# The down product turned round: bf16 passes on bare 4-bit weights, and norm products on either of two engines

## The chip, the cores and the metric

The kernel runs on one core of a Trainium2 chip. The core has five engines, each with its own instruction queue that is worked off strictly in order: TensorE (PE, matrix products; PEld is its weight load), VectorE (DVE), ScalarE (ACT), GpSimd (POOL) and SyncE (SP, which here only starts DMA transfers). They meet through semaphores. The metric is device microseconds (us) of one launch, taken as the median of several runs; smaller is better. Beside the timed runs there is one profiled execution, from which every line of the trace comes.

## The reference

A batch of 16 sequences, 512 tokens of width 512, goes through one attention block and one feed-forward block:

```python
x = x + layernorm(attention(layernorm(x)))      # 16 heads of 32, low-rank q and kv, ALiBi, causal
x = x + layernorm(ffn(layernorm(x)))

def ffn(x):                                     # I = 1408
    w_gu   = fp4_values(gate_up_packed) * scale # [2*I, 512], one scale per 128 inputs and output row
    w_down = fp4_values(down_packed) * scale    # [512, I], one scale per 128 inputs and output row
    gate, up = split(x @ w_gu.T)
    y = (silu(gate) * up) @ w_down.T
    return y / sqrt(mean(y * y) + 1e-6)
```

The weights of the feed-forward block come as 4-bit floating-point values, eight to a 32-bit word, with an fp16 scale for each group of 128 inputs. The 4-bit values (0, 0.5, 1, 1.5, 2, 3, 4, 6 and their negatives) are exact in bf16; the scaled ones are not.

## The kernel before, in words

**Order of the work.** The function builds a list of tasks (`task`, line 77). A task has the engines that may run it, with a cost for each, a due time, and the buffers it reads, writes or holds. `Plan.run` (line 120) then lays all tasks out with a list scheduler: it takes the task that can start first, then the one with the earlier due time, among those due within a window of 0.5 (one unit is one batch) of the next PE task. The result is one fixed order for each engine; nothing is decided on the chip. A task on PE is allowed to start 350 ns after its inputs by the plan's costs. Buffers come from small pools (`SLOTS`, line 270): eight PSUM banks, two `g`, two `u`, two `sum`, two `th` and so on, and a buffer is free again after its last reader in the plan. The plan runs several batches interleaved: while the feed-forward block of batch b is computed, the attention of b+1 and b+2 is.

**Feed-forward block** (`ffn`, line 841). For each of the NI = 11 groups of 128 hidden units, gate and up are computed transposed (hidden units on partitions, 512 tokens along the free side). The normalized input was split in `tail` into three bf16 parts whose sum is the f32 value (`x2`, lines 822 to 833). For each of four input chunks, one PSUM bank gets three bf16 matmuls (one for each part) with the bare 4-bit values as weights (line 859); the bank is scaled as it is read, by ACT (line 873) or by DVE, which also adds (line 880), since the group scale is one number per partition here. POOL adds the two halves (line 886), ACT takes a tanh (line 893), DVE makes the gate (line 896), and POOL multiplies by up into `hT` (line 900), in f32.

The down product then takes `hT` as weights and the scaled f32 `w_dn` as the moving side: for each of four blocks of 128 tokens, 11 f32 matmuls of 128x512 add up in one bank (line 908), so that the result has tokens on partitions:

```python
nc.tensor.matmul(pm.t, h_t.t[:, i, t * P : (t + 1) * P], w_dn.t[:, i, :], ...)
```

Mean and variance of the bank are taken on DVE (`stats`, lines 425 and 426; lines 930 and 931), the root on POOL (lines 446 and 447), and DVE writes the normalized `z` from the bank (line 940). POOL adds it to x (line 945) and starts the store (line 948).

**Norms.** `norm` (line 430) is used three times for a block of tokens: on the input (`xl`), on the attention output read from the bank `pw`, and on x before the feed-forward block. Each ends in a DVE product with mean and root (line 439). With line 940 that is four such products for each of 64 blocks, all on DVE.

**Unpacking** happens once, in the plan of batch 0 (`unpack`, line 489). A DMA copies the words of a group eightfold to partitions, two DVE instructions shift and mask them in place (line 510) in `w_dn`'s own memory. For gate and up, ACT then turns them into bf16 (line 520) and SP stores them to DRAM (`w_gu`), from where each batch loads them again. For down, DVE multiplies with the scales (line 534), which an extra DMA per group brought to all partitions.

Of the kernel before, what the change touches and what calls it, by code (L numbers as in the profile page):

```python
# [12 lines left out]
I32 = mybir.dt.int32  # L13
# [221 lines left out]
def attn_ffn_kernel(  # L235
# [36 lines left out]
        "xl": (NT, [P, D], F32),  # L272
        "x": (2 * NT - 1, [P, D], F32),
        "xnT": (1, [P, ND, L], F32),
# [8 lines left out]
        "x2": (1, [P, 3, ND, L], BF16),  # L283
        "hT": (1, [P, NI, L], F32),
        "g": (2, [P, L], F32),
        "u": (2, [P, L], F32),
        "sum": (2, [P, L], F32),
        "th": (2, [P, L], F32),
# [72 lines left out]
    def load_xl(b, t):  # L361
        xl = xls[b, t] = buf("xl", f"xl_{b}_{t}")
        task(
            {SP: dma(2.6)},
            lambda e: nc.sync.dma_start(xl.t, x_in[b, t * P : (t + 1) * P, :]),
            b - 0.6 + 0.05 * t, writes=[xl],
        )
# [30 lines left out]
    gu = Buf(None, None, "w_gu")  # L398
    w_dn = fixed([P, NI, D], "w_dn")

# [3 lines left out]
    s_gu = fixed([P, NI * NGU], "s_gu")  # L404
    task({SP: dma(3.0)}, lambda e: nc.sync.dma_start(raw.t.bitcast(F16)[:, : NI * NGU], gus), -0.34, writes=[raw])

    def make_scales(e):
        nc.gpsimd.tensor_scalar(s_gu.t, raw.t.bitcast(F16)[:, : NI * NGU], 1.0, None, ALU.mult)
        ups = s_gu.t.rearrange("p (i c) -> p i c", c=NGU)[:, :, ND:]
        nc.gpsimd.tensor_scalar(ups, ups, 0.5, None, ALU.mult)  # L410

    task({POOL: (700.0, 800.0)}, make_scales, 0.1, reads=[raw], writes=[s_gu])


# [15 lines left out]
    def norm(dst, src, rd, wr, tag, due, dur):  # L430

        st, mv, f = stats(src, tag, due)
        task({DVE: (700.0 + 150, 1000.0)}, f, due, reads=rd, writes=[st, mv])
        r = tiny(1, f"r_{tag}")
        task({POOL: (800.0, 900.0)}, lambda e: rsqrt(r.t, mv.t[:, 1:2], EPS_LN), due,
             reads=[mv], writes=[r])
        task(
            {DVE: dur},
            lambda e: nc.vector.tensor_scalar(
                dst(), src(), mv.t[:, 0:1], r.t, ALU.subtract, ALU.mult  # L440
            ),
            due, reads=[mv, r, *rd], writes=wr,
        )

# [42 lines left out]


    def unpack(packed, rows, cols, at, due):
        n = cols // D  # L490
        words = [(w_dn, at + k) for k in range(n)]
        ap = lambda: w_dn.t[:, at : at + n, :].bitcast(I32).rearrange("p i n -> p (i n)")

# [8 lines left out]
            ),  # L502
            due, writes=words,
        )
        for args in (
            (shl, None, ALU.logical_shift_left),
            (3, -0x72000000, ALU.arith_shift_right, ALU.bitwise_and),
        ):
            task({DVE: dve(cols, -0.15 * cols)},
                 lambda e, args=args: nc.vector.tensor_scalar(ap(), ap(), *args),  # L510
                 due, reads=words, writes=words)
        high = lambda: ap().bitcast(F16).rearrange("p (n two) -> p n two", two=2)[:, :, 1]
        return words, high

    def unpack_gate_up(i):
        due = 0.15 + 0.06 * i
        wi = buf("th", f"wq_{i}")
        words, high = unpack(gup, i * 16, NGU * P, i % (NI // 2) * 2, due)
        task({ACT: act(NGU * P)},
             lambda e: nc.scalar.activation(wi.t.bitcast(BF16), high(), AF.Copy, scale=2.0**14),  # L520
             due, reads=words, writes=[wi])
        task({SP: dma(2.0)}, lambda e: nc.sync.dma_start(w_gu[i], wi.t.bitcast(BF16)), due,
             reads=[wi], writes=[(gu, i)])

    def unpack_down(i):
        due = 0.85 + 0.06 * i
        sc = buf("y", f"sc_{i}")
        task({SP: dma(3.5)},
             lambda e: nc.sync.dma_start(sc.t.bitcast(F16)[:, :D], dns[i : i + 1, :].to_broadcast([P, D])),
             due, writes=[sc])  # L530
        words, high = unpack(dnp, i * 16, D, i, due)
        task(
            {DVE: dve(D)},
            lambda e: nc.vector.scalar_tensor_tensor(
                w_dn.t[:, i, :], high(), 2.0**14, sc.t.bitcast(F16)[:, :D], ALU.mult, ALU.mult
            ),
            due, reads=[*words, sc], writes=words,
        )

# [3 lines left out]
    def first_norm(b, t):  # L543
        due = b - 0.3 + 0.06 * t
        if t == 0:
# [292 lines left out]

    GU, DN = 0.0074, 0.0079

    def ffn(m):
        b = m.b
        h_t = buf("hT", f"hT_{b}")
        at = b + FIRST + STEP * (NG * NT + 6.5)
        for i in range(NI):
# [4 lines left out]
            for half, kind in enumerate("gu"):  # L850
                acc = buf(kind, f"{kind}_{b}_{i}")
                add = buf("sum", f"{kind}2_{b}_{i}")
                for c in range(ND):
# [23 lines left out]
                    else:  # L877
# [21 lines left out]
            task({POOL: pool2(512)},  # L899
                 lambda e, i=i, th=th, u=u: nc.gpsimd.tensor_tensor(  # L900
                     h_t.t[:, i, :], th.t, u.t, ALU.mult),
                 at, reads=[th, u], writes=[(h_t, i)])
        for t in range(NT):
            pm = buf("bank", f"py_{b}_{t}")
            for i in range(NI):
                task(
                    {PE: pe(858)},
                    lambda e, i=i, t=t, pm=pm: nc.tensor.matmul(  # L908
                        pm.t,
                        h_t.t[:, i, t * P : (t + 1) * P],  # L910
                        w_dn.t[:, i, :],
                        start=i == 0,
                        stop=i == NI - 1,
                    ),
                    at, reads=[(h_t, i), (w_dn, i)], writes=[pm],
                )
                at += DN
            st, mv, f = stats(lambda pm=pm: pm.t, f"y_{b}_{t}", at)
# [7 lines left out]
            def g1(e, f=f, mv=mv, rr=rr):  # L926
                f(e)
                mean, var = mv.t[:, 0:1], mv.t[:, 1:2]
                ms, ri = rr.t[:, 0:1], rr.t[:, 1:2]
                nc.vector.scalar_tensor_tensor(ms, mean, mean, var, ALU.mult, ALU.add)  # L930
                nc.vector.scalar_tensor_tensor(ri, ms, EPS_LN, var, ALU.mult, ALU.add)

            task({DVE: (1100.0, 1300.0)}, g1, at, reads=[pm], writes=[st, mv, rr])
            task({POOL: (800.0, 900.0)},
                 lambda e, rr=rr: rsqrt(rr.t[:, 1:2], rr.t[:, 1:2], EPS_LN * EPS_RMS),
                 at, reads=[rr], writes=[rr])
            z, x = buf("th", f"z_{b}_{t}"), m.x[t]
            task(
                {DVE: dve(512, 80)},
                lambda e, z=z, pm=pm, mv=mv, rr=rr: nc.vector.tensor_scalar(  # L940
                    z.t, pm.t, mv.t[:, 0:1], rr.t[:, 1:2], ALU.subtract, ALU.mult),
                at, reads=[pm, mv, rr], writes=[z],
            )
            task({POOL: pool2(512)},
# [101 lines left out]
```

## Time and profile before

| | |
|---|---|
| median of 3 runs | 2723.1 us (2720.8 to 2723.44) |
| profiled execution | 2730.41 us, of which 2728.6 us from the first to the last instruction (its span) |
| mean granted TensorE clock in it | 0.992 |
| PE busy | 2653.2 us |
| DVE busy | 1977.7 us |
| ACT busy | 1364.1 us |
| POOL busy | 1190.2 us |

A busy time is the union of an engine's instructions. For PE it is rougher than for the others, because matmuls overlap in a pipeline and their ends are modelled; the distance from one matmul's start to the next is the better measure of what one costs, and a run of many back to back gives it. In lists of groups, a line has: code line, engine, operation, tiles written and read, shape, count, then busy us and mean ns of one, then the engine's idle time just before such instructions and what ended it.

### The profile page before, as it was taken

The page shows a single profiled execution, that of the slowest core. Times are in us where ns is not written, and L with a number is a line of the kernel's source. Part 1 is how long each engine was busy: PE and PEld are TensorE (multiplying, and loading weights), DVE is VectorE, ACT ScalarE, POOL GpSimd, SP SyncE. Part 2 cuts the span into 40 slices and gives each one's busy share as a digit, 9 for nine tenths or more (in the row PEclk, how much of TensorE's full clock was granted, in tenths as well). Part 3 has the DMA queues.
Part 4 walks back from the last instruction along what each step waited for, and adds up shares of the span by engine and source line. Part 5 has one row for each costly group of instructions (what it writes and reads, how often), then busy time and mean ns, then how long its engine had stood idle before and what let it go on. Part 6 is the DMA issues. An engine that isn't in the chain of part 4 may idle for free.

```text
span 2728.6 us, 44045 instructions
## 1 busy us (share of the span) xinstructions
PE 2653.2 (97%) x14733; PEld 1205.7 (44%) x14904; DVE 1977.7 (72%) x4446; ACT 1364.1 (50%) x3339; POOL 1190.2 (44%) x1328
## 2 busy tenths in 40 slices
PE   7989999999999999999999999999999999999998
PEld 3544444444444444444444444444444444444443
DVE  4887795958868587685866868678686876867673
ACT  5755372644636455363553635546364563645441
POOL 1044453535444354453534435354443544534474
PEclk9999999999999999999999999999999999999999
DMA  6577475674956649375584856738576484846710
GB/s 203 159 179 191 136 208 138 178 188 129 233 130 187 174 144 223 113 194 158 158 214 112 210 147 184 192 107 224 151 195 173 139 212 132 207 130 169 187 39 19
DMA packets 460177, 448.20 MB, mean 164 GB/s; under 512 B 38576, under 2 KB 380464, under 8 KB 452272
## 3 DMA queue, kind: packets, MB, share of 16 engines
q1 hardware_dynamic: 454832, 428.61, 59.6%
q0 software_dynamic: 5120, 16.78, 1.7%
q8 instruction: 118, 1.93, 0.3%
q14 instruction: 107, 0.88, 0.1%
HBM read 267.28 MB, written 178.00 MB: 163 GB/s over the span
## 4 chain that ended last, share of the span: by engine, by line
PE 85%; DMA 10%; DVE 2%; SPq 1%; ACT 1%; issue 1%; POOL 0%; POOLq 0%; DVEq 0%; ACTq 0%
PE py L908 22%; PE pu L859 14%; PE pg L859 13%; PE pw L803 8%; PE pq L561 7%; DMA pT<-pd 7%; PE s L641 6%; PE po L775 6%; PE pv L561 2%; PE pc L561 2%; PE pk L561 2%; DMA pd<-p 1%; PE ptf L455 1%; DMA w_dn<-gup 1%; SPq L755 1%
## 5 line engine op out<-in xcount | busy, mean ns | idle before, releaser
L908 PE MATMUL py<-w_dn,hT 128*128 128x512 f32 x1408 | 698.5, 606 | 0.1
L668 ACT ACTIVATE p<-p,nmx 128x128 f32<-128x128 f32 (+3 forms) x1024 | 564.2, 553 | 255.1 <-DVE nmx L653 234.5
L859 PEld LDWEIGHTS <-wi 128*128 128x128 bf16 x4224 | 402.7, 98 | 584.8 <-issue 168.9
L653 DVE CUSTOM_DVE_ANT_0 p<-s,dist 128x128 f32<-128x128 f32 (+3 forms) x1024 | 442.8, 486 | 157.8 <-PE s L641 155.1
L859 PE MATMUL pu<-x,wi 128*128 128x512 bf16 x2010 | 516.3, 382 | 7.5 <-issue 1.1
L859 PE MATMUL pg<-x,wi 128*128 128x512 bf16 x2043 | 498.7, 380 | 4.4 <-POOL x L831 0.9
L886 POOL TENSOR_TENSOR u<-u,u 128x512 f32<-128x512 f32 x176 | 242.5, 1378 | 487.9 <-DVE u L880 487.1
L748 DVE STREAM_TRANSPOSE p<-p 128x512 f32<-128x512 f32 x240 | 360.0, 1501 | 42.8 <-ACT p L668 42.7
L908 PEld LDWEIGHTS py<-w_dn,hT 128*128 128x128 f32 x1408 | 248.2, 190 | 247.1 <-issue 227.5
L880 DVE SCALAR_TENSOR_TENSOR u<-pu,s_gu,u 128x512 f32<-128x512 f32 x352 | 258.7, 743 | 125.3 <-ACT u L873 73.3
L873 ACT ACTIVATE u<-pu,s_gu 128x512 f32<-128x512 f32 x352 | 240.6, 685 | 214.3 <-PE pu L859 204.4
L880 DVE SCALAR_TENSOR_TENSOR g<-pg,s_gu,g 128x512 f32<-128x512 f32 x352 | 258.7, 740 | 96.0 <-ACT g L873 50.7
L873 ACT ACTIVATE g<-pg,s_gu 128x512 f32<-128x512 f32 x352 | 240.0, 683 | 144.3 <-PE pg L859 126.5
L886 POOL TENSOR_TENSOR g<-g,g 128x512 f32<-128x512 f32 x176 | 233.9, 1329 | 143.5 <-DVE g L880 142.3
L900 POOL TENSOR_TENSOR hT<-th,u 128x512 f32<-128x512 f32 x176 | 224.9, 1278 | 95.4 <-DVE th L896 89.8
L561 PE MATMUL pq<-xnT,w_q 128*128 128x512 f32 x512 | 233.3, 598 | 1.5 <-ACT w_q L416 1.5
L803 PE MATMUL pw<-w_o,atT 128*128 128x512 f32 x512 | 230.2, 593 | 0.0
L775 PE MATMUL po<-pT,v 128*32 128x128 f32 x5120 | 193.5, 278 | 30.5 <-DMA pT<-pd 28.9
L641 PE MATMUL s<-kT,qT 32*128 32x128 f32 (+3 forms) x2048 | 216.2, 487 | 1.8 <-ACT qT L583 1.7
L775 PEld LDWEIGHTS po<-pT,v 128*32 128x32 f32 x5120 | 125.8, 109 | 159.8 <-issue 98.0
L668 ACT ACTIVATION_READ_ACCUMULATOR p<-p,nmx 128x1 f32 x1024 | 194.6, 190 | 0.0
L803 PEld LDWEIGHTS pw<-w_o,atT 128*128 128x128 f32 x512 | 97.0, 190 | 122.7 <-issue 119.7
(87 smaller groups left out, 2341.4 us busy)
## 6 DMA issues: line engine op xcount, KB each, us to landing
pd<-p SPq DMA_DIRECT2D x60, 1024.0 KB
pT<-pd SPq DMA_DIRECT2D x240, 256.0 KB
pd<-p SPq DMA_DIRECT2D x60, 768.0 KB
pT<-pd SPq DMA_DIRECT2D x240, 192.0 KB
wi<-w_gu SPq DMA_DIRECT2D x176, 256.0 KB
pd<-p SPq DMA_DIRECT2D x60, 512.0 KB
pT<-pd SPq DMA_DIRECT2D x240, 128.0 KB
xl<-x_in SPq DMA_DIRECT2D x64, 256.0 KB
```

Of the source, the lines that this page charges most:

```text
L561: nc.tensor.matmul(pm.t, lhs(c), rhs(c), start=c == 0, stop=c == n - 1)
L641: nc.tensor.matmul(s[j].t[:, :w], q.t[rows, qb * P : (qb + 1) * P], k.t[rows, :w], start=True, stop=True,)
L653: lambda e, j=j: nc.vector.tensor_tensor_reduce(part(m, p, j), runs(s[j].t[:, :w]), runs(dist.t[:, L - w :]), -SLOPES[g * HPG + j], 3.4e38 ...
L668: lambda e, j=j: nc.scalar.activation(part(m, p, j), part(m, p, j), AF.Exp, bias=nmx.t[:, j : j + 1], scale=-1.0, accum_out=sums.t[:, qb * ...
L748: task({DVE: dve(row, 0.07 * row)}, lambda e: nc.vector.transpose(flat(p.t), flat(p.t)), due, reads=[p], writes=[p])
L775: nc.tensor.matmul(po.t[j * HD : (j + 1) * HD, qb * P : (qb + 1) * P], m.v.t[:, kb, h * HD : (h + 1) * HD], p_t.t[:, kb, :, j, :], start=k ...
L803: nc.tensor.matmul(pm.t, m.at.t[:, g, t * P : (t + 1) * P], w_o.t[:, g, :], start=g == 0, stop=g == NG - 1,)
L859: nc.tensor.matmul(pm.t, wi.t[:, o * P : (o + 1) * P], m.x2.t[:, n, c, :], start=n == 0, stop=n == 2,)
L873: lambda e, to=to, pm=pm, s=s: nc.scalar.activation(to.t, pm.t, AF.Copy, scale=s),
L880: lambda e, to=to, pm=pm, s=s: nc.vector.scalar_tensor_tensor(to.t, pm.t, s, to.t, ALU.mult, ALU.add),
L886: lambda e, acc=acc, add=add: nc.gpsimd.tensor_tensor(acc.t, acc.t, add.t, ALU.add),
L908: lambda e, i=i, t=t, pm=pm: nc.tensor.matmul(pm.t, h_t.t[:, i, t * P : (t + 1) * P], w_dn.t[:, i, :], start=i == 0, stop=i == NI - 1,),
```

## The change

The down product is done like gate and up. The output is kept transposed: for each hidden group i and each of four blocks of 128 outputs, one bank takes three bf16 matmuls, with the bare 4-bit values of `w_dn` (now bf16) as weights and the three bf16 parts of the hidden values (`h3`) as the moving side. `split` makes those parts from `u` in four steps: cast (ACT or DVE), subtract (DVE or POOL), cast, subtract. A bank no longer adds over i; it is scaled as it is read and added to `acc` in SBUF: by ACT for i = 0, by DVE with the sum in one instruction for odd i, by ACT to a buffer and then a POOL add for the other even i. When all 11 groups are in, `acc` is turned back by f32 transposes on PE into a bank for each block of tokens, and the norm follows as before.

The products at the end of all norms may be done by DVE or by ACT (`scaled`); for ACT a POOL instruction more (`shift`) makes minus mean times root. Unpacking uses two buffers of the pool `acc`, ACT makes the bf16 values for down as well, its due time is earlier, and its scales come in one DMA instead of eleven. Pools: `hT` is gone; `acc` (2) and `h3` (2) are new, `u` has 3, `sum` 4, `x` 8. The first norm and its load have earlier due times.

```diff
-        "x": (2 * NT - 1, [P, D], F32),
+        "x": (2 * NT, [P, D], F32),
...
-        "hT": (1, [P, NI, L], F32),
+        "acc": (2, [P, ND, L], F32),
+        "h3": (2, [P, 3, L], BF16),
-        "u": (2, [P, L], F32),
-        "sum": (2, [P, L], F32),
+        "u": (3, [P, L], F32),
+        "sum": (4, [P, L], F32),
...
-            b - 0.6 + 0.05 * t, writes=[xl],
+            b - 0.8 + 0.05 * t, writes=[xl],
...
-    w_dn = fixed([P, NI, D], "w_dn")
+    w_dn = fixed([P, NI, D], "w_dn", BF16)
...
+        scaled(dst, src, mv, r, rd, wr, due, dur)
+
+    def shift(r, mv):
+        nc.gpsimd.tensor_scalar(r[:, 1:2], mv[:, 0:1], r[:, 0:1], -1.0, ALU.mult, ALU.mult)
+
+    def scaled(dst, src, mv, r, rd, wr, due, dur):
+        def f(e):
+            if e == ACT:
+                nc.scalar.activation(
+                    dst(), src(), AF.Identity, bias=r.t[:, 1:2], scale=r.t[:, 0:1])
+            else:
+                nc.vector.tensor_scalar(
+                    dst(), src(), mv.t[:, 0:1], r.t[:, 0:1], ALU.subtract, ALU.mult)
+        task({DVE: dur, ACT: act(512, 80)}, f, due, reads=[mv, r, *rd], writes=wr)
...
-    def unpack(packed, rows, cols, at, due):
-        words = [(w_dn, at + k) for k in range(n)]
+    def unpack(packed, rows, cols, name, due, dst, wr, hold=()):
+        words = buf("acc", name)
...
+        task({ACT: act(cols)},
+             lambda e: nc.scalar.activation(dst(), high(), AF.Copy, scale=2.0**14),
+             due, reads=[words], writes=wr)
...
     def first_norm(b, t):
-        due = b - 0.3 + 0.06 * t
+        due = b - 0.5 + 0.06 * t
...
+    def split(u, h3, due):
+        def minus(dst):
+            return {DVE: dve(512, 60), POOL: pool2(512)}, lambda e, n: (
+                nc.vector if e == DVE else nc.gpsimd
+            ).tensor_tensor(dst(), u.t, h3.t[:, n, :], ALU.subtract)
+        for n in range(2):
+            task(either(512), lambda e, n=n: copy(e, h3.t[:, n, :], u.t), due,
+                 reads=[u], writes=[(h3, n)])
+            on, f = minus((lambda: u.t) if n == 0 else (lambda: h3.t[:, 2, :]))
+            task(on, lambda e, n=n, f=f: f(e, n), due, reads=[u, (h3, n)],
+                 writes=[u if n == 0 else (h3, 2)])
+
+    def down(b, i, h3, acc, due):
+        for o in range(ND):
+            pm = buf("bank", f"pd_{b}_{i}_{o}")
+            def f(e, o=o, pm=pm):
+                for n in range(3):
+                    nc.tensor.matmul(pm.t, w_dn.t[:, i, o * P : (o + 1) * P],
+                                     h3.t[:, n, :], start=n == 0, stop=n == 2)
+            s = s_dn.t[:, i * ND + o : i * ND + o + 1]
+            due += GU
+            add = buf("sum", f"y2_{b}_{i}_{o}") if i > 0 and i % 2 == 0 else None
+            task({PE: pe(648)}, f, due, reads=[(w_dn, i), h3], writes=[pm], ...)
+            if add is None and i > 0:
+                task({DVE: dve(512, 80)}, ... scalar_tensor_tensor(y(), pm.t, s, y(), ALU.mult, ALU.add))
+                continue
+            task({ACT: act(512, 80)}, ... activation(to(), pm.t, AF.Copy, scale=s))
+            if add is not None:
+                task({POOL: pool2(512)}, ... tensor_tensor(y(), y(), add.t, ALU.add))
...
-                     h_t.t[:, i, :], th.t, u.t, ALU.mult),
+            task({POOL: pool2(512)},
+                 lambda e, th=th, u=u: nc.gpsimd.tensor_tensor(u.t, th.t, u.t, ALU.mult), ...)
+            h3 = buf("h3", f"h3_{b}_{i}")
+            split(u, h3, at)
+            down(b, i, h3, acc_y, at + 12 * GU)
+            at += ND * GU
         for t in range(NT):
             pm = buf("bank", f"py_{b}_{t}")
-            for i in range(NI):
-                task({PE: pe(858)}, ... matmul(pm.t, h_t[:, i, t], w_dn[:, i, :]) ...)
+            def f(e, t=t, pm=pm):
+                for o in range(ND):
+                    nc.tensor.transpose(pm.t[:, o * P : (o + 1) * P],
+                                        acc_y.t[:, o, t * P : (t + 1) * P], ident)
+            task({PE: pe(4 * 109)}, f, at + 0.1, reads=[acc_y], writes=[pm])
```

## The prediction

> **What bounds the kernel now.** I read the page first: busy times, the 40 slices, the chain that ended last.
>
> ```profile
> span 2728.6 us, 44045 instructions
> ...
> PE 2653.2 (97%) x14733; PEld 1205.7 (44%) x14904; DVE 1977.7 (72%) x4446; ACT 1364.1 (50%) x3339; POOL 1190.2 (44%) x1328
> ...
> PE   7989999999999999999999999999999999999998
> ...
> DVE  4887795958868587685866868678686876867673
> ...
> PE 85%; DMA 10%; DVE 2%; SPq 1%; ACT 1%; issue 1%; POOL 0%; POOLq 0%; DVEq 0%; ACTq 0%
> ```
>
> PE is full in every slice but the first three and the last, and the chain is PE for 85%. DVE has 28% to spare on average, ACT half. A change is thus worth what it takes from PE, until another engine makes PE wait. Does anything do so today? The list of waits, by engine:
>
> ```profile
> PE po L775 <- DMA pT<-pd: 28.9, 23, 3.5
> ...
> DVE w_dn L510 <- DMA w_dn<-gup: 24.9, 6, 9.2
> ...
> PEld s L641 <- DVE p L748: 19.2, 26, 0.8
> ```
>
> The only wait of PE itself of any size is the attention's DMA turn, 28.9 us in 23 places. No wait of PE's matmuls on DVE, ACT or POOL stands high in that list; the largest of its weight loads on DVE (last line, us in total, times, longest) is 19.2 us in pieces below 1. The middle line is the start-up: DVE stands 24.9 us for unpacking words.
>
> The price of a matmul comes from the chain in order of time, at the end of the last batch, where PE runs undisturbed:
>
> ```profile
> 2629.24 2.59 PE pu L859 x12
> ...
> 2678.45 36.92 PE py L908 x86
> ...
> 2718.99 2.45 POOL x L945 x2
> ```
>
> Twelve bf16 matmuls of 128x512 in 2.59 us: 0.2158 each, 0.648 a bank. An f32 matmul of that size is two records: 36.92/43 = 0.859. Last, the groups that the new work resembles:
>
> ```profile
> L908 PE MATMUL py<-w_dn,hT 128*128 128x512 f32 x1408 | 698.5, 606 | 0.1
> ...
> L880 DVE SCALAR_TENSOR_TENSOR u<-pu,s_gu,u 128x512 f32<-128x512 f32 x352 | 258.7, 743 | 125.3 <-ACT u L873 73.3 <-PE pu L859 39.6 <-ACT th L893 6.0
> ...
> L886 POOL TENSOR_TENSOR g<-g,g 128x512 f32<-128x512 f32 x176 | 233.9, 1329 | 143.5 <-DVE g L880 142.3
> ...
> L896 DVE SCALAR_TENSOR_TENSOR th<-th,g 128x512 f32<-128x512 f32 x176 | 137.6, 782 | 2.8 <-ACT th L893 2.6
> ...
> L831 POOL TENSOR_TENSOR x<-xr,x 128x512 bf16<-128x512 f32 x64 | 75.7, 1183 | 59.0 <-ACT x L416 45.3 <-DVE x L416 13.6
> ```
>
> **PE, step by step.** Removed: 16 batches x 11 groups x 4 blocks = 704 f32 matmuls x 0.859 = 604.5 us. Added: 704 banks x 3 = 2112 bf16 matmuls x 0.2158 = 455.8 us; their weight loads (98 ns on line 859) go beside a matmul of 216, as for gate and up. Added: 64 x 4 = 256 f32 transposes. The timeline prices one:
>
> ```profile
> 2601.39 0.60 PE L455 MATMUL ptf<-ident,y 128*128 128x128 f32 x4
> ...
> 2601.83 0.59 PE L908 MATMUL py<-w_dn,hT 128*128 128x512 f32 x1
> ```
>
> Four take 0.44 us until the next matmul starts, 0.11 each, so 28.2 us. [...] PE: -604.5 + 455.8 + 28.2 = **-120.5 us**. Weight loads, switches between matmul shapes and the attention are as many as before within some per cent (889 changes of shape against 909 in the two orders), at nothing.
>
> **Is the new work on DVE, ACT and POOL hidden?** Counts are from the order of the changed kernel, where the plan's choices stand. DVE gets 320 bank reads x 0.735 (258.7/352) = +235, 109 casts x 0.43 = +47, 119 subtractions x 0.67 = +80, some other copies +16; it loses 173 of 256 norm products (0.60 to 0.81 each) = -130 and the scaling of down, -7. Sum +241: 2219 us. ACT gets 384 bank reads x 0.685 = +262, 243 casts x 0.59 = +143, 173 products = +116, rest -5: 1880. POOL gets 320 adds x 1.33 = +425, 233 subtractions x 1.2 = +280, 256 `shift` x 0.235 = +60: 1955. Against a span near 2640 that is 84%, 71% and 74%: all below PE, but DVE and POOL far nearer to it than before. Early on it is tightest: in the first 500 us, every other stretch of 80 us of PE work carries some 83 us of DVE against about 86 us that PE really takes for it.
>
> The two also share a port. One timeline shows it:
>
> ```profile
> 1208.25 1.27 POOL L886 TENSOR_TENSOR u<-u,u 128x512 f32<-128x512 f32 x1 [7.53 <-DVE u L880]
> ...
> 1208.68 1.39 DVE L896 SCALAR_TENSOR_TENSOR th<-th,g 128x512 f32<-128x512 f32 x1
> ```
>
> The DVE instruction, whose two inputs lie in SBUF, ends 0.55 after the POOL one it met, so 0.69 of work took 1.39. On average line 896 pays 0.10 (782 ns against some 682 undisturbed) while POOL is busy 44%. [...] From the row, 0.10 x 74/44 = 0.17 each: 80 us, of which 29 were there before. The row is measured in this mix, where work that depends on each other seldom collides; I take +51 us on DVE (2270, 86%), and about as much on POOL.
>
> What of that reaches PE? The chain behind one group's last bank is: DVE read 0.74, POOL add 1.33, POOL product 1.28, cast 0.59, subtract 0.67 to 1.28, cast 0.59, subtract 0.67 to 1.18: 5.9 to 7.0, with six hand-overs of some 0.1 about 7 us. In the order, PE has between that bank and the first bank of its down product a median of 14.7 us of other work (gate and up of later groups, attention), and 10 us or more except in the last groups of the run. So the cover is 3 us at worst, 8 typically. If the cover were gone, each us of lateness costs 176 us. I put 0.1 us a group: **+18** (bounds 0 and 170). What is late next is then whatever stands behind that bank in PE's queue: gate and up, scores, and the DMA turn that follows scores.
>
> **Both ends of the run.** The last batch has no cover. After the last gate bank PE has four down banks (2.6 us) against a chain of 6.3: 3.7 idle. Then four banks, ACT 0.68 and four POOL adds in a row, 5.2: PE idles 4.2. Then all four token blocks come at once: statistics 1.25, and POOL has four roots (1.03 with `shift`), four adds of 1.23, stores of 0.6; with one wait for ACT about 19.6 us from the turn to the end, where today 13.2 us follow PE's end at 2715.4. **+14** (8 to 25). At the start, 22 unpackings pass through two buffers instead of eleven groups' places; a buffer comes round after its DMA, which took 5.5 us (34.83 to 40.39 us), and attention starts behind three such rounds. I take one to two rounds' difference, **+8** (bounds -5, as eleven scale loads and DVE's scalings go from SP and DVE, and +30). SP's queue is otherwise the same, and the extra `x` buffer costs nothing.
>
> **Sum.** 2728.6 - 120.5 + 18 + 14 + 8 = 2648 for the span; the median of the runs lies 5.5 below the span, so **2643 us**, 2.9% faster.
>
> **Rivals.**
> 1. *As summed*, 2643, own range 2598 to 2690: PE has no waits on DVE today.
> 2. *The cover is too thin: slower.* The split chain comes late in the steady state, PE stands at the first down bank of each group, and gate, up and scores stand behind it. For: DVE at 86%, POOL at 78%, orders fixed by costs that know nothing of the port, and four more hand-overs between in-order queues. Against: a median cover of 14.7 us for a chain of 7. It decides from 0.5 us of waiting a group ((2723 - 2643)/176 beyond what I allowed); at 1 us, 2800.
> [...]
> 4. *DMA takes it.* The turn's wait of 28.9 us grows if PE reaches `po` sooner; DMA engines are 89% busy in the densest stretch. Doubling it gives 2672, inside 1.
> 5. *bf16 passes dearer than for gate and up*: same shape, same weight loads, so I see no reason; 2112 x 0.03 would be +63, 2706.
>
> **How the numbers follow.** Case 1 with 4: 0.65. Cases 3 and 5, 2690 to 2718: 0.10, all faster but the last part, of which 0.03 falls within 0.2% of 2723.1 (about what a measurement of this kernel can tell from no change: 2717.7 to 2728.5). Case 2: 0.25, nearly all slower, mostly 2730 to 2850. Faster 0.72, same 0.04, slower 0.24. To leave no more than 2 in 10 out, the range runs from 2595 (start and stalls at nothing) to 2745.
>
> **What would show it.** Right: PE still 95% or more, down banks 2112 records at 216 spacing, the group of the removed line gone, DVE near 2270 and POOL near 2030 busy, waits of PE on DVE or POOL for `h3` below 40 us, 20 us or so of idle PE at the end. Wrong: a large "PE pd waits for DVE or POOL" in the list of waits, DVE or POOL at a tenth of 9 in most slices, PE below 92%; or subtractions on DVE with means near 1.2 us.

## The result, and the profile after

The changed kernel takes **2763.5 us** (median of 4 runs, 2758.4 to 2766.1) where the kernel before takes 2723.3 on the same chip: a ratio of 1.014 (95% interval 1.0122 to 1.0157). It is 1.4% slower, and the whole interval lies above 1; forecast were 2643 us and a range up to 2745. The rows of its page that answer to those of before:

```profile
span 2761.5 us, 48331 instructions
...
PE 2588.1 (94%) x15631; PEld 1211.6 (44%) x15864; DVE 2353.3 (85%) x4830; ACT 1842.2 (67%) x4130; POOL 1947.6 (71%) x2138
...
PE   8999999999999999999999999999999999998885
...
PE 60%; DVE 10%; POOL 9%; DMA 9%; issue 5%; SPq 3%; ACT 2%; POOLq 0%; DVEq 0%; ACTq 0%
```

PE still shows 9 in nearly every slice, so the slices alone would hide what happened. Two rows give it away: the chain that ended last is PE for 60% where it was 85%, and the mean granted clock fell from 0.992 to 0.976. The slice digit counts a matmul at half clock as busy (from 985.00 to 988.40 us PE is busy for all 3.40 us, at a clock of 0.50). The waits (us in total, times, longest):

```profile
PE po L779 <- DMA pT<-pd: 40.2, 29, 3.2
PEld s L645 <- DVE nmx L657: 23.9, 27, 1.3
PEld pta L472 <- DVE g L936: 20.5, 13, 1.6
...
PE pta L472 <- DVE g L936: 14.1, 13, 1.1
PE pd L866 <- DVE h L850: 13.4, 11, 3.0
PE po L779 <- DVE g L936: 13.3, 13, 1.1
...
PE pd L866 <- DVE h L423: 6.4, 4, 2.7
```

Before, no row of PE's own waits on DVE was above 8 us. Now DVE is named in most rows. Only the last row and the fifth are the split chain that the forecast had followed, and most of their time (all but 3.8 us of the 19.8) falls after 2580 us, in the last batch and just ahead of it. The first row is the attention's DMA turn: its probabilities go through DRAM (`pd` there, not the bank `pd` of the down product) and come back transposed. `pta` (transposes of the input) and `po` (the attention's last product) wait for a bank that DVE has not read yet (`g`, line 936), each once in 13 batches. DVE's groups say why it is late (the first line is of the kernel before):

```profile
L931 DVE SCALAR_TENSOR_TENSOR rr<-rr,mv_y 128x1 f32<-128x1 f32 x64 | 10.2, 159 | 2.2
...
L952 DVE SCALAR_TENSOR_TENSOR th<-th,g 128x512 f32<-128x512 f32 x176 | 198.8, 1130 | 26.8 <-ACT th L949 26.7
L423 DVE CAST h<-u 128x512 bf16<-128x512 f32 x109 | 103.6, 951 | 14.4 <-POOL u L956 12.6 <-POOL u L850 0.2
L850 DVE TENSOR_TENSOR h<-u,h 128x512 bf16<-128x512 f32 x74 | 81.9, 1107 | 0.7 <-ACT h L423 0.2
...
L988 DVE SCALAR_TENSOR_TENSOR rr<-rr,mv_y 128x1 f32<-128x1 f32 x64 | 36.8, 575 | 2.2
```

The gate product (line 896 before) went from a mean of 782 ns to 1130. An instruction on one column per partition, line 988 (line 931 before), took 159 ns before and takes 575 now: no work of its own can explain that.

What stands ahead of the bank reads on which PE waits can be looked up. At all 13 waits of `po` for `g` it is a gate product that took 3.3 us or more; at all 13 of `pta` it is line 988, at 1.09 us each time; it begins 0.08 us after a POOL subtraction (line 850) and ends within 0.02 us of that one's end. The first of the `po` waits (start, us, engine and line):

```profile
330.78 0.75 POOL L1002 DMA_DIRECT2D out<-x  x1
...
331.17 3.46 DVE L952 SCALAR_TENSOR_TENSOR th<-th,g 128x512 f32<-128x512 f32 x1
...
331.57 1.27 POOL L942 TENSOR_TENSOR u<-u,u 128x512 f32<-128x512 f32 x1
...
332.80 1.27 POOL L999 TENSOR_TENSOR x<-x,z 128x512 f32<-128x512 f32 x1
...
335.34 0.43 PE L779 MATMUL po<-pT,v 128*32 128x128 f32 x8 [1.14 <-DVE g L936]
```

The gate product begins beside POOL's store, and the two adds that POOL starts after it both take their usual 1.27 us; it ends 0.56 us after the second, the bank read behind it in DVE's queue takes 0.74, and PE has stood 1.14 us. So at these two places it isn't the split's own instructions that are late, but ones that the kernel before has too, held by POOL.

**Where the 32.9 us of span come from.** For each profile I added up PE's gaps (time from one matmul's start to the next beyond the spacing of its kind, 0.216, 0.109, 0.429 us), the time that the clock lost (span times one minus the mean granted clock), and what follows PE's last end. "Period" is the time from one batch's first `pw` to the next one's, in the middle of the run.

| | before | after | difference |
|---|---|---|---|
| PE's own work, by the forecast's sum | | | -120.5 |
| PE's gaps | 93.6 | 192.3 | +98.7 |
| lost clock | 21.8 | 66.3 | +44.5 |
| after PE's last end | 12.4 | 18.7 | +6.3 |
| sum, against the span's +32.9 | | | +29.0 |
| period of a batch | 165.6 | 166.6 | +1.0 |

Gaps and lost clock overlap where PE stands at half clock (some 3 us more than before lie after PE's end alone), and missing records (line 866 shows 2051 of its 2112 matmuls) blur the gaps; the account is good to some 20 us. PE's idle time as the profile counts it, a cruder measure, rises by nearly as much, from 63.0 to 154.7 us. The message doesn't hang on the 20 us: PE's work got shorter, and more than it saved came back as standing and as slow clock.

The clock can be read in stretches of the changed kernel (length, then busy us and count of PE, PEld, DVE, ACT, POOL, then the granted clock, DMA share, GB/s):

```profile
981.00:983.10 2.10, 0.09 (x4) 0.12 (x8) 2.10 (x7) 1.75 (x4) 1.85 (x5) 0.63 1.22 190
983.10:985.00 1.90, 1.68 (x18) 0.97 (x20) 0.66 (x4) 0.08 (x1) 0.46 (x1) 0.50 0.64 236
985.00:988.40 3.40, 3.40 (x24) 2.00 (x27) 0.74 (x2) 2.81 (x7) 2.04 (x2) 0.50 0.28 81
```

PE stands 2.2 us for the DMA turn, and then works 5.3 us at half clock. There were 25 such stretches, most of them one to a batch, against 10 before.

### The profile page after: what moved, and what is told of

Its sections match the earlier page's. It is cut to its first block, busy times and chain, and to the rows that moved or that the text cites. A ratio compares the mean times of both kernels' runs of the same rounds, so it can differ in the third digit from the quotient of the medians.

```text
span 2761.5 us, 48331 instructions
## 1 busy us (share of the span) xinstructions
PE 2588.1 (94%) x15631; PEld 1211.6 (44%) x15864; DVE 2353.3 (85%) x4830; ACT 1842.2 (67%) x4130; POOL 1947.6 (71%) x2138
## 4 chain that ended last, share of the span: by engine, by line
PE 60%; DVE 10%; POOL 9%; DMA 9%; issue 5%; SPq 3%; ACT 2%; POOLq 0%; DVEq 0%; ACTq 0%
PE pd L866 11%; PE pg L915 11%; PE pu L915 11%; DMA pT<-pd 6%; PE pq L565 6%; PE pw L807 5%; PE po L779 5%; PE s L645 4%; SPq L759 3%; DVE p L657 2%; POOL u L956 2%; PE pc L565 2%; PE pv L565 1%; DVE g L936 1%; PE pk L565 1%
## 5 line engine op out<-in xcount | busy, mean ns | idle before, releaser
L866 PE MATMUL pd<-h,w_dn 128*128 128x512 bf16 x2051 | 538.8, 393 | 29.3 <-DVE h L850 13.4
L915 PE MATMUL pg<-x,wi 128*128 128x512 bf16 x2009 | 509.2, 381 | 10.2 <-DVE u L936 1.5
L893 POOL TENSOR_TENSOR acc<-acc,y 128x512 f32<-128x512 f32 x320 | 424.4, 1340 | 50.0 <-ACT y L888 49.6
L866 PEld LDWEIGHTS <-w_dn 128*128 128x128 bf16 x2112 | 202.1, 100 | 323.5 <-issue 139.1
L888 ACT ACTIVATE y<-pd,s_dn 128x512 f32<-128x512 f32 x320 | 212.9, 685 | 124.7 <-PE pd L866 108.4
L942 POOL TENSOR_TENSOR u<-u,u 128x512 f32<-128x512 f32 x176 | 233.2, 1325 | 65.2 <-DVE u L936 63.7
L956 POOL TENSOR_TENSOR u<-th,u 128x512 f32<-128x512 f32 x176 | 227.6, 1293 | 59.0 <-DVE th L952 56.4
L779 PE MATMUL po<-pT,v 128*32 128x128 f32 x5120 | 200.5, 285 | 59.7 <-DMA pT<-pd 40.2
L645 PE MATMUL s<-kT,qT 32*128 32x384 f32 (+3 forms) x2048 | 238.9, 481 | 7.6 <-DVE nmx L657 7.4
L882 DVE SCALAR_TENSOR_TENSOR acc<-pd,s_dn,acc 128x512 f32<-128x512 f32 x320 | 220.3, 741 | 6.9 <-PE pd L866 3.7
```

The lines of the kernel that those rows point to most:

```text
L645: nc.tensor.matmul(s[j].t[:, :w], q.t[rows, qb * P : (qb + 1) * P], k.t[rows, :w], start=True, stop=True,)
L866: nc.tensor.matmul(pm.t, w_dn.t[:, i, o * P : (o + 1) * P], h3.t[:, n, :], start=n == 0, stop=n == 2,)
L893: lambda e, y=y, add=add: nc.gpsimd.tensor_tensor(y(), y(), add.t, ALU.add),
L915: nc.tensor.matmul(pm.t, wi.t[:, o * P : (o + 1) * P], m.x2.t[:, n, c, :], start=n == 0, stop=n == 2,)
L942: lambda e, acc=acc, add=add: nc.gpsimd.tensor_tensor(acc.t, acc.t, add.t, ALU.add),
```

## The experiments

Two theories were set against each other. **P, the port:** DVE's casts, subtractions and gate products wait for POOL's instructions; DVE is late, so PE is late. ("Port" is the prediction's name for it and stays a name: the traces show the wait, as in the 1.39 us for 0.69 of work at 1208.68 us of the trace of before, and not what the two share.) **O, the order:** the fixed order expects inputs, the DMA turn above all, earlier than they come. Not all runs were made side by side: the kernel before took 2723.3 to 2728.5 us beside them, so a difference of two rows below is good to about 5 us. PE's gaps are by the sum explained above. Every line number below is of the kernel named, and shifts by a few with an edit.

| kernel | us | ratio to before (95%) | clock | PE's gaps, us | of these, `po` for the DMA turn |
|---|---|---|---|---|---|
| changed kernel | 2763.5 | 1.014 (1.0122, 1.0157) | 0.976 | 192 | 45 |
| before, less PE work | 2606.5 | 0.9558 (0.9535, 0.9582) | 0.992 | | |
| before, norms either | 2728.6 | 1.0001 (0.9993, 1.001) | 0.995 | | |
| norms on DVE | 2761.2 | 1.0129 (1.0105, 1.0153) | 0.974 | 205 | 88 |
| POOL short | 2706.5 | 0.9925 (0.99, 0.9949) | 0.984 | 142 | 78 |
| POOL writes | 2740.6 | 1.0052 (1.0036, 1.0068) | 0.972 | 167 | 65 |
| split short on DVE | 2728.2 | 0.9998 (0.9987, 1.0009) | 0.982 | 170 | 51 |
| port told to the planner | 2702.9 | 0.9915 (0.9898, 0.9931) | 0.982 | 136 | 49 |
| order with slack | 2714.2 | 0.9966 (0.995, 0.9982) | 0.984 | 144 | 7 |
| split off DVE | 2662.1 | 0.9766 (0.9751, 0.978) | 0.988 | 110 | 16 |
| split off DVE, DMA later | 2656.3 | 0.9737 (0.9719, 0.9755) | 0.987 | 103 | 7 |
| split off DVE, order with slack | **2647.9** | 0.9705 (0.9689, 0.972) | 0.988 | 111 | 6 |
| two parts | 2670.7 | 0.9797 (0.9777, 0.9818) | 0.970 | 256 | 63 |

### Was the kernel before bound by PE at all?

The kernel before, with two of the eleven groups left out of its down product (its output lacks them): 128 f32 matmuls, 110 us of PE less, all else as it was.

```diff
             for i in range(NI):
+                if i >= NI - 2:
+                    at += DN
+                    continue
...
-                        stop=i == NI - 1,
+                        stop=i == NI - 3,
```

> The kernel before, with the down product over 9 of 11 groups (the last two are left out): 128 f32 matmuls less, 110 us of PE, nothing else less but their waits. If PE alone bounds the kernel before, as I read it: 2613 to 2630. If another loop (the DMA turn of the attention, or DVE) has the same period: above 2680.

121 us came off, a little more than the PE work and than the range for this reading. So PE did bound it, its DMA turn and its DVE could go at the faster pace, and the first step of the forecast stands: a microsecond taken from PE was worth a microsecond there.

### The norm products: worth nothing either way

In the changed kernel, all norm products back on DVE, and `shift` gone:

```diff
-        task({DVE: dur, ACT: act(512, 80)}, f, due, reads=[mv, r, *rd], writes=wr)
+        task({DVE: dur}, f, due, reads=[mv, r, *rd], writes=wr)
```

> The changed kernel with all norm products on DVE again, without the extra POOL instruction. Theory P (DVE is what is late): 173 products come back to DVE, some 125 us, and the time rises to 2790 or more. Rival N (the products on ACT wait for POOL and are late, holding banks): it falls to 2745 or less.

And that part alone, put into the kernel before:

> The kernel before with one part of the change alone: norm products on ACT or DVE, the shift on POOL; the down product is as before. Before is bound by PE, so both theories: within 0.3% of before, 2716 to 2732, DVE down by some 100 us, ACT up by about as much. Beyond that on the slow side, the part costs something by itself (POOL's longer root, a later xnT).

2761.2 against 2763.5, and 2728.6 against 2728.5: both within the measurement. In the first neither theory's range came: DVE rose by 52 us to 2404.9, and the time did not, so DVE's sum alone does not set it. In the second, DVE went from 1977.7 to 1852.7 us and ACT from 1364.1 to 1494.2, and nothing followed. The loss is in the rest of the change: the down product, with the unpacking, the buffers and the due times that came with it. These three were not tested apart from it.

### POOL short, in the same order

The planner sees the same costs, so PE, DVE and ACT have the same instructions in the same order. Only POOL's two-input instructions for the hidden values and for `acc` work on 8 columns of 512 (with a fill behind those that write bf16), so most of each result is left out.

```diff
+    def pool_op(dst, a, b, op):
+        nc.gpsimd.tensor_tensor(dst[:, :8], a[:, :8], b[:, :8], op)
+        if dst.dtype == BF16:
+            nc.gpsimd.memset(dst[:, 8:], 0.0)
```

> The order of PE, DVE and ACT is that of the changed kernel. The POOL instructions of the feed-forward block (adding halves, product with up, adding to acc, subtractions) work on 8 of 512 columns; the rest is left out. Theory P (POOL's length and its hold on the shared port make DVE late, and DVE makes PE late): the gate product on DVE falls from 1130 ns to near 690, and the time falls by 70 us or more, to 2690 or less. Rival O (the fixed order is slow by itself, through DVE's and ACT's own work): 2745 or more.

2706.5: 57 us better than the changed kernel. DVE, whose instructions are untouched, is busy 2157.7 us instead of 2353.3. Its groups:

```profile
L957 DVE SCALAR_TENSOR_TENSOR th<-th,g 128x512 f32<-128x512 f32 x176 | 120.4, 684 | 32.4 <-ACT th L954 32.4
L853 DVE TENSOR_TENSOR h<-u,h 128x512 bf16<-128x512 f32 x74 | 51.8, 699 | 0.6 <-ACT h L423 0.2
L423 DVE CAST h<-u 128x512 bf16<-128x512 f32 x109 | 45.9, 422 | 0.4
```

1130 became 684, 1107 became 699, 951 became 422. So **196 us of DVE's time was waiting for POOL**. But the time fell to neither theory's range, and not to 2643. PE's gaps for DVE nearly went (71 to 13 us in my sum), and those for the DMA turn grew (45 to 78):

```profile
PE po L779 <- DMA pT<-pd: 72.4, 50, 5.9
```

With DVE on time, the next input that this order expects too early shows up. P is right about DVE, and it is not the whole. This kernel takes two things away, POOL's hold on DVE and POOL's own length; the next one parts them.

### POOL as long, but only writing

As the last one, but each POOL instruction is followed by two that fill the other 504 columns with counted numbers, so that POOL is busy as long as in the changed kernel (1942.5 us) and reads little.

```diff
+        for _ in range(2):
+            nc.gpsimd.iota(dst[:, 8:], pattern=[[1, L - 8]], base=1, channel_multiplier=1,
```

> The same order and the same short POOL instructions, each followed by two iotas that fill the other columns, so that POOL is busy about as long as in the changed kernel but reads SBUF only for a moment (the values are not the right ones). If it is the port's read side that makes DVE late: the DVE instructions with two SBUF inputs are short again and the time is within 20 us of the run with short POOL instructions. If it is POOL's own length, in a chain behind which PE waits: 2745 to 2765, like the changed kernel.

```profile
L958 DVE SCALAR_TENSOR_TENSOR th<-th,g 128x512 f32<-128x512 f32 x176 | 119.5, 679 | 37.0 <-ACT th L955 36.9
...
L423 DVE CAST h<-u 128x512 bf16<-128x512 f32 x109 | 53.9, 494 | 22.7 <-POOL u L848 21.8
```

2740.6, in neither range. The gate product stays at 679 ns, DVE at 2165.4 us. So it isn't POOL's being busy that holds the gate product up (1130 ns in the changed kernel, with POOL at 1947.6 us), it is its reading. The subtractions, which have two inputs as well, are at 694 to 716 ns. For the casts, which have one input, writing is enough to hold them a little: of 31 that began beside a fill, 24 took 0.57 to 0.83 us, against 0.42 undisturbed.

The times part what the shorter POOL gave: 23 us from the changed kernel to this one, where DVE is freed of nearly all its waits and POOL is as long as ever (each of its instructions is three), and 34 from here to the last one, where POOL is short. By this, in the unchanged order, the waits at the port are worth 23 us. Most of the second part shows in the profiles as clock: PE's idle time by the profile is 117 us here and 110 there, the lost clock 77 and 43 (the execution profiled here took 2751.8 us).

### The split short on DVE: a failed relief that measures the wait

DVE's own 109 casts and 119 subtractions on 8 columns, the rest of `h3`'s part a fill; all orders as in the changed kernel. The output lacks those columns.

```diff
+    def short(dst, a, b=None, op=None):
+        if b is None:
+            nc.vector.tensor_copy(dst[:, :8], a[:, :8])
+        else:
+            nc.vector.tensor_tensor(dst[:, :8], a[:, :8], b[:, :8], op)
+        if dst.dtype == BF16:
+            nc.vector.memset(dst[:, 8:].bitcast(F32), 0.0)
```

> The changed kernel, every engine with the same instructions in the same order, but DVE's own 109 casts and 119 subtractions of the split work on 8 of the 512 columns (the rest of h3's part is a short fill, so h is wrong and the output with it). ACT's casts and POOL's subtractions stay whole, POOL stays as long as it is. It separates what the split costs on DVE from what a new plan brings (the kernel with the split taken off DVE was planned anew). DVE: casts 0.89 and subtractions 1.14 each become some 0.1 to 0.3, so 230 us less the fills' 35: 2353 -> near 2160, as in the kernel with the split off DVE. Theory P (DVE late by its split instructions that wait for POOL at the port, everything else follows): 2670 to 2700, stalls of PE on DVE near what they are there, the gate product still over 1.0 us each. Theory O (the fixed order expects inputs too early): 2730 to 2760, PE's waits moving to the DMA turn, 65 us or more of it. Near 2706 (as with POOL shortened) would be both: about half the loss from DVE, the rest from the order.

2728.2, between the two ranges, and DVE fell by 50 us only, to 2302.9. As a test of the two theories it fails, because it did not do what it was for: a cast of 8 columns keeps 0.67 of its 0.95 us, and a subtraction half of its own.

```profile
L848 DVE CAST h<-u 128x8 bf16<-128x8 f32 x109 | 73.2, 672 | 14.4 <-POOL u L964 12.6 <-POOL u L856 0.2
L850 DVE TENSOR_TENSOR h<-u,h 128x8 bf16<-128x8 f32 x74 | 42.5, 575 | 0.3 <-ACT h L423 0.2
L850 DVE TENSOR_TENSOR u<-u,h 128x8 f32<-128x8 f32 x45 | 27.9, 619 | 6.1 <-ACT h L423 6.0
```

The timeline shows one (start, us, engine and line):

```profile
1011.64 1.26 POOL L950 TENSOR_TENSOR g<-g,g 128x512 f32<-128x512 f32 x1
1011.71 1.23 DVE L848 CAST h<-u 128x8 bf16<-128x8 f32 x1
```

It starts 0.07 after POOL's and ends 0.04 after it. Of the 228, 56 met no running POOL instruction and took 0.149 on average; 172 met one and took 0.787. Over all it is 0.630, so **the port costs 0.48 us for each such instruction**. At 512 columns it is much the same: from the changed kernel to the one with POOL short, a cast lost 0.53, a subtraction 0.41 to 0.47, a gate product 0.45.

### The split taken off DVE

ACT does all casts, POOL all subtractions; the planner makes a new order. Nothing is left out.

```diff
-            return {DVE: dve(512, 60), POOL: pool2(512)}, lambda e, n: (
+            return {POOL: pool2(512)}, lambda e, n: (
...
-            task(either(512), lambda e, n=n: copy(e, h3.t[:, n, :], u.t), due,
+            task({ACT: act(512)}, lambda e, n=n: copy(e, h3.t[:, n, :], u.t), due,
```

> The changed kernel, planned anew with the casts of the split on ACT alone and its subtractions on POOL alone: DVE loses 228 instructions, and nearly all of what the split made it wait at the shared port. Theory P (DVE's waits at the port make PE late): 2725 or less. Theory O (PE waits because the fixed order expects inputs, and above all the DMA turn, earlier than they come, whichever engine is late): 2745 to 2775.

**2662.1**, 101 us below the changed kernel, 2.3% below before; the period of a batch is 158.4. POOL is busier than ever (2039.7 us), DVE at 2172.1. The gate product still takes 947 ns (684 with POOL short), so the port is relieved and not free. This changes two things at once, DVE's waits and the order, so it does not say which of them gave how much.

### The planner told of the port, or given slack

Two kernels leave the split open to both engines, as in the changed kernel, and change only what the planner believes. In the first, a subtraction, cast or gate product on DVE costs 0.3 to 0.5 us more; in the second, PE is planned no sooner than 1.5 us after an input from another engine (0.35 before) and a DMA lands 3.0 us after its transfer (1.0 before).

```diff
-            return {DVE: dve(512, 60), POOL: pool2(512)}, lambda e, n: (
+            return {DVE: dve(512, 530), POOL: pool2(512)}, lambda e, n: (
...
-            task({DVE: dve(512, 60)},
+            task({DVE: dve(512, 480)},
```

> The changed kernel with the costs that the plan uses for DVE raised to what the trace of the changed kernel shows: 1.1 us for a subtraction and for the gate product, 0.9 for a cast. Work and instructions are the same; which engine takes a cast or a subtraction, and the order, follow the plan. If the order is bad because it doesn't know of the port: 2735 or less. If not: 2750 or more.

```diff
-    LANDED = 1000.0
+    LANDED = 3000.0
...
-                hop = 0.0 if d.eng == e else self.SLACK if e == PE else self.HOP
+                hop = 0.0 if d.eng == e else 1500.0 if e == PE else self.HOP
```

> The changed kernel with another order alone: the plan lets a PE task start 1.5 us after its inputs instead of 0.35, and 3 us after a landed DMA instead of 1, so that PE's queue has other work ahead of late inputs. Work, engines' choices apart, is the same. Theory O: PE's waits for the DMA turn (43 us) and for DVE (50 us) shrink to half, with them the stretches at half clock: 2700 to 2730. Theory P: DVE and POOL stay as late, and the time stays at 2750 or more.

2702.9 and 2714.2: 61 and 49 us better than the changed kernel. In the first, the dearer DVE was also given less: 13 casts, 11 subtractions and 29 norm products fewer, and DVE fell to 2276.0 us, so it is not the order alone. The second is the clean one: DVE has 2 casts, 7 subtractions and 5 norm products more and is as slow as ever, 2371.1 us, its 111 casts at a mean of 1361 ns, and the DMA turn has all but gone from the waits:

```profile
PE po L779 <- DMA pT<-pd: 6.7, 4, 2.5
```

PE's idle time for DVE stayed as it was, 65 us by the profile. So O holds as well: with the port's waits untouched, another order alone was worth 49 us, and the DMA turn is most of what it covered.

### Both

The same slack, and a smaller one that concerns only the DMA turn (2.0 us), on top of the split taken off DVE:

> The same, with 3.0 us for a DMA and with PE planned at least 1.5 us (not 0.35) after its inputs from other engines. The planner's own length grows by 14 us over the kernel with the split off DVE, so PE's planned waits grow while its unplanned ones fall. Theory O: 2640 to 2660, PE stalls below 90 us in all. Theory P: slower by the planned slack, 2665 to 2680.

> The kernel with the split off DVE, planned anew with one number changed: the planner takes a DMA's data as landed 2.0 us (not 1.0) after its transfer. Nothing is left out. There PE still waits 110 us, 15 of them for the DMA turn, 15 for the up product's DVE read. Theory O: the turn's waits go to near 5, and each removes a stretch of half clock behind it: 2640 to 2655. Theory P: nothing changes at DVE, 2655 to 2670.

**2647.9** and 2656.3. The second lies just above O's range, with 7 us of the turn's waits left. The first is the fastest kernel with the whole work, 3.0% below before, and its page reads much as the forecast had wanted the changed kernel's to read:

```profile
PE 2543.3 (96%) x15622; PEld 1189.4 (45%) x15864; DVE 2128.9 (80%) x4616; ACT 1877.4 (71%) x4225; POOL 2048.6 (77%) x2257
...
PE 75%; ACT 7%; POOL 6%; DVE 5%; issue 3%; DMA 3%; SPq 1%; POOLq 0%; DVEq 0%; ACTq 0%
```

Its period is 158.0 us, 7.6 less than before; the 120.5 us of PE work that the forecast took off make 7.5 a batch.

Together with the kernels above it makes a square:

| | planned without slack | planned with slack |
|---|---|---|
| split on DVE and POOL | 2763.5 | 2714.2 |
| split on ACT and POOL | 2662.1 | 2647.9 |

Slack is worth 49 where the split is on DVE too, and 14 where it isn't and DVE waits less; taking the split off DVE is worth 101 without slack, 66 with it. So the two causes don't add: as far as four kernels can say, each of them costs more where the other is there. Every plan gives another order, so no row or column changes one thing alone.

The planner's own idea of the time, by its costs and not the chip's, is no measure here. It puts the end of the changed kernel at 2612.7 us, of the kernel with the split off DVE at 2625.3, of that with slack at 2638.9. On the chip their spans are 2761.5, 2655.9 and 2648.7, the other way round (the third plan is longer partly because the slack counts in it).

### Is PE still the bound of the changed kernel?

Two bf16 parts instead of three in the down product (the third part of the hidden values is left out), so 704 matmuls, 152 us of PE, and half of the split are gone; split on both engines as in the changed kernel.

```diff
-                for n in range(3):
+                for n in range(2):
                     nc.tensor.matmul(
```

> The changed kernel with two bf16 parts of the hidden values instead of three: 704 bf16 matmuls less (152 us of PE), and a cast and a subtraction less for each group (some 80 us on ACT and DVE, 170 on POOL and DVE). The result is a little less exact. If PE's load still counted one to one: 2610. If the waits set the time, as in steady state where the period stayed at 166 us: by theory P about 2680, since DVE and POOL lose load; by theory O above 2690.

2670.7: 93 us for 152 of PE and half of the split, and no faster than the kernel with three parts and the split off DVE. PE's gaps are 256 us in it:

```profile
PE po L779 <- DMA pT<-pd: 58.5, 43, 4.0
PE pg L913 <- DVE atT L793: 52.1, 12, 4.8
```

The gaps grew by 64 us: PE's load no longer counts one to one, and a good part of what is taken from it turns into waits. The kernel before gave more than all of 110 us back. The time lies near what was expected of P and under the range of O.

## Why the prediction was wrong, step by step

**PE, -120.5: about right.** The down banks run at 0.216 a matmul and the transposes 0.109 apart, as priced; the mean duration of a transpose in the trace of before, 281 ns on line 455, would have been 44 us too much in the sum. If I subtract gaps and lost clock from PE's time, its own work fell by 97 to 116 us, depending on the kernel, in an account that is good to some 20. The period of the fastest kernel, 7.6 us below that of before, agrees.

**The port, +51 on DVE: the first step that failed.** I took 0.17 us for each of 471 DVE instructions (176 gate products, 119 subtractions, 109 casts, 67 norm products on SBUF), 80 us in all, scaled from the gate product's mean in the trace of before by POOL's busy share; that it was not more I argued from "work that depends on each other seldom collides". No run shows the 0.17. Measured by making POOL short: 0.40 each for the same 471, and 31 us more for 128 instructions on one column, of which I had not thought. DVE's busy time, in which overlapping records count once, fell by 196 us in all, where I had 80. What did not carry over is how often the two meet. In the trace of before, POOL was running at the start of 46 of the 176 gate products (POOL busy 44%); in the changed kernel, of 145 (71%), and those that waited did so for longer (34 of them for 0.53 us each before, 88 for 0.90 after). DVE came to 2353 and not 2270, although its own work was some 30 us less than I had summed (2219 without the 29 of waits already there, against 2157.7). POOL paid too, but less than the "about as much" that I expected: its two-input instructions on 512 columns take 1.27 us undisturbed (1.16 for a bf16 result or a subtraction), and beyond that they waited 35 us in all before and 64 in the changed kernel.

**The cover, +18: the step that turned the sign.** I compared the split chain, 7 us, with the PE work ahead of the first down bank, 14.7, and found cover. For that chain this was right in all but the last batch: between the first `pw` of the second batch and that of the last, PE stood 5 us for `h`. What I did not follow was DVE's queue. Once in each of 13 batches a gate product held for 3.3 us, and once a line 988 held for 1.09, stood ahead of bank reads, and `po` and `pta` waited for these banks. PE's gaps for DVE rose from 10 to 71 us, those for the DMA turn from 30 to 45. I had named that turn as "what is late next", and had a price for it in rival 4 only. With the port's waits removed and POOL as long as it was, 23 us came back; the remainder has to do with POOL's length and with an order that leaves late inputs uncovered.

**No step at all for the clock: +44.** Around the transposes the clock is full in the trace of before (1.00 at 2601 us, where they were priced). What a stall does to the clock afterwards had no cost in the sum. It added nearly half again to what the stalls cost.

**The end, +14; the start, +8.** From the last batch's first `pw` to the end it is 170.7 us against 140.1, so +31. PE's idle time in this stretch rose from 2.9 to 27.4 us, 18.6 of it for `h`, and what follows PE's end by 6.3, which is what I had for that part. So the end was too small by some 17 us, in the waits of the batch without cover. It is no matter of the port alone: the fastest kernel stands 33.6 us there. The start measured +2.4 (the first scores of batch 1 begin at 118.4 us against 116.0).

**The rivals.** Rival 2, "the cover is too thin: slower", had the right sign, at 0.25, and by its price the point of decision: 99 us more in gaps over 176 groups is 0.56, which is where its own sum meets no change; the clock did the rest. Its mechanism was half right: not the first down bank of each group, but banks behind DVE's queue. Case 3, DVE taking over in part (2690 to 2718 together with case 5), had the right engine: DVE came to 2353 us against the 2270 of the sum. It let half of the gain go where more than all of it went, because it asked only whether DVE's sum exceeds PE's, and not what its lateness does in a fixed order. Rival 4 took place on a smaller scale (the turn's gaps grew by 15 us, not by 28.9), rival 5 didn't come.

**What stays open.** How the 116 us between the changed kernel and the fastest one divide between port and order cannot be said; the square shows that they don't add. In the unchanged order, the port alone is worth 23 us by the kernel whose POOL only writes, and together with POOL's length 57. Why the DMA turn's waits grow from 45 to 78 us when DVE is relieved was not followed to its end. The smaller parts of the change, its buffers, due times and unpacking, have no run of their own.

## What to carry to other kernels

Where DVE and POOL both read SBUF as here, an estimate for each DVE instruction with two SBUF inputs, and for each plain cast, is its own time plus half of a POOL instruction times POOL's busy share: from the changed kernel's trace 0.5 x 1.27 x 0.71 = 0.45 us, where 0.40 to 0.48 was measured in that order. Don't scale it from a row in which the two seldom met. Loading POOL made DVE's old instructions late too, down to those on one column (line 988, 159 to 575 ns). When an in-order engine gets more to do or to wait for, follow what stands behind it in that queue, not only the chain of the moved work: a bank read a microsecond late stopped PE for as long (1.14 us at 335.34 us). And before a saving on PE is counted, ask whether the order has slack for it; here, allowing inputs from other engines 1.15 us more in the plan and landed DMAs 2 us more was worth 49 us with nearly the same instructions on each engine.

## What the runs showed of the hardware, unexpected

A wait of DVE for POOL had no relation to the size of the waiting instruction: a cast of 8 columns took 1.23 us beside a POOL add of 1.26. Nor was it bounded by one POOL instruction: a gate product that began beside a store stood through two POOL adds that began after it, and took 3.46 us for 0.68 of work. Writing alone did not hold up the instructions with two inputs: with POOL just as busy (1942.5 us), but filling instead of reading, the gate product was back at 679 ns. It did hold up a cast, 0.64 us on average beside a fill against 0.42 alone.

In the changed kernel the clock fell after little idling. Half clock came in stretches of 3.41 us or multiples of it (but for the one that the end of the trace cuts off), and all 25 begin on one grid of 3.413 us. In the 3.41 us ahead of such a stretch, PE had stood between 0.5 and 3.4 us. Those with 0.5 came at the same place in nine batches, in a window filled mostly by scores, whose matmuls are 32*128 in the list of groups where those of the other products are mostly 128*128; elsewhere windows with up to 1.97 us of standing kept the full clock. So how long PE stood does not decide it alone. What does can't be told from these runs, only the bill: 44 us, nearly half as much as the additional gaps themselves.
